# A transformer decoder on Trainium2: VectorE's and ScalarE's instruction orders fixed by hand in the attention stages, and side work placed anew

## The chip, the cores and the metric

The kernel runs on one core of one Trainium2 chip. The core has five engines that run their own instruction streams: TensorE (PE in the profile) multiplies matrices, VectorE (DVE) and ScalarE (ACT)[...], GpSimd (POOL) works on the large on-chip memory (SBUF), and SyncE (SP) issues transfers. TensorE's results land in PSUM[...]. The metric is the device time of one execution in microseconds (us); lower is better.

## The reference, cut to what matters

All numbers are fp32. The input `x` is 8 batches of 256 tokens of width 256. Six blocks are added to it, one after the other; the change touches the first four.

```python
x = x + self_attention_0(layernorm(x))        # 16 heads of 16, rotary q and k, biases
x = x + cross_attention_0(ctx, layernorm(x))  # queries are layernorm(x) itself, keys and values are
                                              # halves of ctx; keys beyond the batch's length masked
x = x + experts_0(layernorm(x))               # below
x = x + self_attention_1(layernorm(x))        # 16 heads of 16, rotary, causal
x = x + cross_attention_1(layernorm(x), ctx)  # 16 heads of 64, projections, a null key
x = x + experts_1(layernorm(x))               # top-1 gate of 8 experts of width 704, a shared one

def experts_0(x):                             # for each batch alone
    g = clip(x @ gate, 1e-6)                  # 256 tokens x 8 experts
    for _ in range(8):                        # sinkhorn, here without the logarithm
        g = g / g.sum(tokens); g = g / g.sum(experts)
    vals, idx = top_k(g.T, 32)                # each expert takes its 32 best tokens
    out[idx[e]] = (x[idx[e]] @ W[e]) * vals[e]   # scattered back; the last expert's entry stands
```

## The kernel before, in words

**Units and steps.** The stage that the change touches takes the first 548 us. It is cut into 24 units (L759 to L768). Units 0 to 15 go by pairs of batches: two `SelfAttention` of layer 0, then two `CrossAttention`. Units 16 to 23 are the causal `SelfAttention` of layer 1, one for each batch. Each unit has four steps: two halves `c` of the heads by two tiles `kt` of 128 keys. The main loop (L905 to L926) goes over units `n` and steps `k`. In each pass it calls `scores` of the next step, then `values` of this one, then the side work listed for `(n, k)`. TensorE runs the matmuls in just this order.

**A step.** `scores` makes four matmuls into `st`, whose PSUM pool `scp` has one buffer of four banks. Two exponentials on ScalarE then turn it into `pT` (L339); the next step's `st` can start only when both have read it. In the causal layer GpSimd sets half of each `pT` to zero behind the diagonal (`affine_select`, L344). `values` makes eight matmuls into `o` (L365). After an odd step `divided_T` (L385) runs on VectorE: a transpose to `by_q`, a reciprocal of the sums `dens`, a multiplication, a transpose into `attT`.

**What a self-attention unit needs around its steps.** `norm` takes statistics on VectorE, `rs` by a power on GpSimd (L258), and writes the two halves of `xn` on VectorE. `rows` transposes `xn` on TensorE (`tr`, L285), and ScalarE copies it to `xnT`. `heads(t)` projects half the tokens (`qk`) and turns q and k: VectorE multiplies by cosines (`qc`) and sines (`qs`, two instructions). In layer 0 GpSimd adds the turned bias to `qc`. The sum of `qc` and `qs` goes to `qkr`: for t=0 on GpSimd, for t=1 on VectorE (L460). `vals(t)` projects `v`, which ScalarE copies into `padv`. `begin` transposes `qkr`: keys (`tr`, copied by ScalarE to `kT`) and queries (`qps`, L472). `masked_queries` (L303) then writes `qps` twice with heads masked in turn: one half of `qm` on VectorE (L306), one on ScalarE (L307). `out(t)` projects `attT` (`ao`) and adds it to `x` on VectorE; in layer 0 GpSimd adds `offset` to `x` first. The side lists put all this one or two units ahead: for unit n, `norm` at (n-2, 2), `rows` at (n-2, 3), both `heads` at (n-1, 0), both `vals` at (n-1, 1), `begin` at (n-1, 2); `out` follows in unit n+1.

**What a cross-attention unit needs.** `norm` at (n-1, 0); GpSimd's copies of the values, `vals`, at (n-1, 1); `begin`, which transposes `xn` into `qps` and masks it, at (n-1, 2). `out` (`oR`) transposes `attT` back and adds it to `x`.

**The experts.** For each pair of batches the generator `chosen_experts` (L621) does the third block. It is advanced one piece at a time by `experts_at` (L846), whose numbers are pieces per step; the pair of units 4i to 4i+3 is treated in units 4i+5 to 4i+10, the last two pairs in fewer (13 to 17 and 16 to 20). Its pieces: rows normalised to `xnb` and transposed; logits `lg`; eight sinkhorn rounds (`cs` on TensorE, L649, then five small VectorE instructions that end at `g`, L659); the top 32 in four rounds of MAX8, FIND_INDEX8 and MATCH_REPLACE8 on VectorE (L670 to L674), written to DRAM and read back; `pick` on GpSimd (L699), `rps` on TensorE, a copy to `rT`; the expert matmuls `y`; `put` on GpSimd, `junk`, `weight` and `ys` on VectorE; `back` on TensorE, added to `x`.

**What sets the order.** [...] Only TensorE's order is the one written:

```python
order.enter_context(tc.manual_schedule(engines={mybir.EngineType.PE}))
```

For VectorE, ScalarE, GpSimd and SyncE a scheduler, when the program is built, picks the next instruction by its own estimate of what is ready and by priority. Five places raise the priority with `tc.high_priority(offset=SOON)`: the norms, `divided_T`, the experts' norms and the sinkhorn rounds. All small products share three PSUM buffers in the pool `mm` (L558).

**Start and end.** Before the loop come unit 0's `norm`, `turn` (the turned biases), `rows`, `heads` and `vals`, unit 1's `norm`, `load`, `key_tables`, `begin`, unit 1's `rows` and the first `scores`. At unit 1 `expert_tables` (L591) loads the experts and writes zeros to buffers in DRAM: `xs`, `ys`, `yo` and eight times a part of `packs`, all from GpSimd's queue. After (20, 3) `weights_x` (L772) loads 6 MB for the fifth block. After the loop `tables_x` (L797) makes small tables, among them `nvw`, and then comes the last unit's `out`.

Of the kernel before, what the change touches and what calls it, by code (L numbers as in the profile page):

```python
# [39 lines left out]
P = 128  # L40
# [17 lines left out]
SOON = 60  # L58
# [99 lines left out]
def plain(  # L158
# [144 lines left out]
    def masked_queries(work, ps, masks):  # L303

        qm = work.tile([P, 2, 2, S], F32, tag="qm", name="qm")
        nc.vector.tensor_scalar(qm[:, :, 0, :], ps, masks[:, 0:1], None, ALU.mult)  # L306
        nc.scalar.activation(qm[:, :, 1, :], ps, AF.Copy, scale=masks[:, 1:2])  # L307
        return qm

    class Core:  # L310
# [9 lines left out]
        def scores(self, step):  # L320


            c, kt, q0 = self.queries(step)
            n = S - q0
            st = scp.tile([P, 4, 2, S], F32, tag="sc", name="st")
            for r in range(4):
                rows = slice(HP * r, HP * r + HP)
                nc.tensor.matmul(  # L328
                    st[:, r, :, :n],
                    self.kT[rows, c, bass.ts(kt, P)],  # L330
                    self.qm[rows, c, :, q0:],
                    start=True,
                    stop=True,
                )
            pTs = []
            for k in range(2):
                pT = work.tile([P, 2, 2, S], F32, tag="pT", name="pT", bufs=4)
                kb = {} if self.bias is None else {"bias": self.bias[:, kt : kt + 1]}
                nc.scalar.activation(  # L339
                    pT[:, :, :, :n], st[:, 2 * k : 2 * k + 2, :, :n], AF.Exp, scale=self.scale, **kb  # L340
                )
                if self.causal:

                    nc.gpsimd.affine_select(  # L344
                        out=pT[:, :, :, :P],
                        in_=pT[:, :, :, :P],
                        compare_op=ALU.is_ge,
                        fill=0.0,
                        base=0,
                        pattern=[[0, 2], [0, 2], [1, P]],  # L350
                        channel_multiplier=-1,
                    )
                pTs.append(pT)
            self.exps[step] = pTs

        def values(self, step):
# [22 lines left out]
            if kt:  # L379
                with tc.high_priority(offset=SOON):  # L380
                    divided_T(self.attT[:, c, :], o, self.dens[:, c, :])
# [47 lines left out]
    class SelfAttention:  # L429
# [8 lines left out]

        def norm(self):
            with tc.high_priority(offset=SOON):  # L440
                self.xn = work.tile([P, 2, D], F32, tag="xn", name="xn")
                mv, rs = norm_stats([x[:, 2 * self.b + t, :] for t in range(2)], 1e-5, small, "ln")
                for t in range(2):
                    self.head = normed(self.xn[:, t, :], x[:, 2 * self.b + t, :], mv, rs, t)
# [9 lines left out]
        def heads(self, t):  # L454
            qk = mm.tile([P, 2 * D], F32, tag="mm", name="qk")
            self.projected(qk, t, 0, 2 * D)
            qc, qs = rotary(qk, t, self.layer, work)
            if self.bias is not None:
                nc.gpsimd.tensor_tensor(qc, qc, self.bias[0][:, t, :], ALU.add)
            (nc.vector if t else nc.gpsimd).tensor_tensor(self.qkr[:, t, :], qc, qs, ALU.add)  # L460
# [15 lines left out]

        def out(self, t):
            b, attT = self.b, self.core.attT
            xt = x[:, 2 * b + t, :]
            if self.bias is not None:  # L480
                nc.gpsimd.tensor_tensor(xt, xt, self.bias[1], ALU.add)
# [31 lines left out]
    class CrossAttention:  # L513
# [12 lines left out]

        def norm(self):
            with tc.high_priority(offset=SOON):
                self.xn = work.tile([P, 2, D], F32, tag="xn", name="xnx")
                mv, rs = norm_stats([x[:, 2 * self.b + t, :] for t in range(2)], 1e-5, small, "ln")  # L530
                for t in range(2):
                    normed(self.xn[:, t, :], x[:, 2 * self.b + t, :], mv, rs, t)
# [88 lines left out]
    def chosen_experts(b0, nb):  # L621
# [3 lines left out]
        def normed_rows(b):  # L625
            with tc.high_priority(offset=SOON):
                mv, rs = norm_stats([x[:, 2 * (b0 + b) + t, :] for t in range(2)], 1e-5, small, "ln")
                for t in range(2):
                    normed(xn[:, 2 * b + t, :], x[:, 2 * (b0 + b) + t, :], mv, rs, t)

        normed_rows(0)
        yield
        for b in range(nb):
            xnT = transposed(xn[:, 2 * b : 2 * b + 2, :], work, mm, "xnT")
# [6 lines left out]
            if b + 1 < nb:  # L641
                normed_rows(b + 1)
# [3 lines left out]
        for it in range(8):  # L646
# [3 lines left out]
            with tc.high_priority(offset=SOON):  # L650
                rc = bwork.tile([P, nb, E], F32, tag="rc", name="rc")
                nc.vector.reciprocal(rc, cs)
                nc.vector.tensor_tensor(g, g, rc.unsqueeze(2).to_broadcast([P, nb, 2, E]), ALU.mult)
                rsum = bwork.tile([P, nb, 2], F32, tag="rsum", name="rsum")
                nc.vector.tensor_reduce(rsum, g, AX.X, ALU.add)
                rr = bwork.tile([P, nb, 2], F32, tag="rr", name="rr")
                nc.vector.reciprocal(rr, rsum)
                dst = gt.rearrange("p t b e -> p b t e") if it == 7 else g
                nc.vector.tensor_tensor(dst, g, rr.unsqueeze(3).to_broadcast([P, nb, 2, E]), ALU.mult)  # L659
# [10 lines left out]
        for r in range(0, TOP, 8):  # L670
            nc.vector.max(top[:, 1, r : r + 8], v)
            nc.vector.max_index(place[:, r : r + 8], top[:, 1, r : r + 8], v)
            if r + 8 < TOP:
                nc.vector.match_replace(v, top[:, 1, r : r + 8], v, NEG)  # L674
        nc.vector.tensor_copy(top[:, 0, :], place)
# [162 lines left out]
    sides = {(n, k): [] for n in range(len(units)) for k in range(4)}  # L838

    def beside(n, k, *made):  # L840
        if n >= 0:
            sides[n, k] += made

    ex = [chosen_experts(2 * i, 2) for i in range(B // 2)]

    def experts_at(i, n, *counts):  # L846
        for k, m in enumerate(counts):
            beside(n, k, *[lambda: next(ex[i], None)] * m)

    for n, u in enumerate(units):  # L850
        if u.__class__ is SelfAttention:
            beside(n - 2, 2, u.norm)
            beside(n - 1, 0, partial(u.heads, 0), partial(u.heads, 1))
            beside(n - 1, 1, partial(u.vals, 0), partial(u.vals, 1))
            beside(n - 1, 2, u.begin)
            beside(n - 2, 3, u.rows)
            if u.layer:
                beside(n + 1, 2, partial(u.out, 0)) if n + 1 < len(units) else None
                beside(n + 1, 3, partial(u.out, 1)) if n + 1 < len(units) else None
            else:  # L860
                beside(n + 1, 0, partial(u.out, 0), partial(u.out, 1))
    for n, u in enumerate(units):
        if u.__class__ is CrossAttention:
            beside(n - 1, 0, u.norm)
            beside(n - 1, 1, u.vals)
            beside(n - 1, 2, u.begin)
            beside(n + 1, 0 if n == 15 else 2, u.out)
    beside(0, 1, add_up)
    beside(3, 3, slot_tables)
    for i in range(3):  # L870
        n = 4 * i + 5
        experts_at(i, n, 2, 2, 1, 1)
        experts_at(i, n + 1, *((1, 2, 2, 2) if i == 2 else (1, 1, 1, 1)))
        experts_at(i, n + 2, *((0, 1, 0, 0) if i == 2 else (0, 1, 1, 1)))
        if i < 2:
            experts_at(i, n + 3, 1, 0, 0, 1)
            experts_at(i, n + 4, 0, 1, 1, 1)
            experts_at(i, n + 5, 0, 1, 1, 1)
        else:
            experts_at(i, n + 3, 1, 1, 1, 1)  # L880
            experts_at(i, n + 4, 0, 1, 1, 1)
    experts_at(3, 16, 1, 1, 1, 1)
    experts_at(3, 17, 1, 2, 2, 2)
    experts_at(3, 18, 1, 1, 1, 0)
    experts_at(3, 19, 0, 1, 1, 2)
    experts_at(3, 20, 1, 2, 0, 0)

    units[0].norm()
    opening = ExitStack()
    opening.enter_context(tc.issue_after(units[0].head.ins))  # L890
    turn()
    order = ExitStack()
    order.enter_context(tc.manual_schedule(engines={mybir.EngineType.PE}))
    units[0].rows()
    for t in range(2):
        units[0].heads(t)
        units[0].vals(t)
    units[1].norm()
    for u in units[:2]:
        u.load()  # L900
    key_tables()
    units[0].begin()
    units[1].rows()
    units[0].core.scores(0)
    for n, u in enumerate(units):  # L905
# [8 lines left out]
        for k in range(4):  # L914
            if k < 3:
                u.core.scores(k + 1)
            elif n + 1 < len(units):
                units[n + 1].core.scores(0)
            u.core.values(k)
            for made in sides[n, k]:  # L920
                made()
            if (n, k) == (20, 3):
# [4 lines left out]
    wn, nvw, hot8 = tables_x(wd, wq_x, wout_x, nkrow, nvcol)  # L927
    order.close()
    for t in range(2):
        units[-1].out(t)  # L930
    first.close()
# [1881 lines left out]
```

## Time and profile before

| | |
|---|---|
| median of 3 runs | 1289.84 us (1289.42 to 1290.94) |
| profiled execution | 1294.03 us |
| its span, first to last instruction | 1292.3 us |
| mean TensorE clock granted | 0.971 of full |
| TensorE busy | 1171.2 us, 91% |
| VectorE, ScalarE, GpSimd busy | 582.7, 438.2, 374.4 us |
| first score matmul, last score matmul | 29.5 us, 529.4 us |
| first matmul of the next stage (`fm`) | 548.4 us |

The profile covers one execution. Busy time counts an engine's own work, not its waits; work of several engines overlaps, so the columns don't add to the span. In the table of stretches, each line begins with the window in us from the start and its length; then come the busy times of PE, PE's weight loads, DVE, ACT and POOL, each with a count of instructions, then the granted TensorE clock, the share of transfers, and GB/s. In the list of waits, a line names the instruction that waited, the one it waited for, and then the total in us, the count and the longest. In a timeline a line has the start and the duration in us, the engine, the source line, the operation, what it writes and reads (partitions by elements), how many instructions were put together, and in brackets the idle time before and what ended it.

### The profile page before, as it was taken

To read this page: it belongs to the slowest core of one execution; us is meant where nothing else is said; L and a number is where in the kernel's file an instruction comes from. 1 tells how busy PE (TensorE), PEld (TensorE's weight loads), DVE (VectorE), ACT (ScalarE), POOL (GpSimd) and SP (SyncE) were. 2 spreads that over 40 slices of the span, in tenths; PEclk is the share of its full clock that TensorE was granted. 3 is DMA by queue.
4 is the path that set the end of the run, shared out by engine and by line. 5 is a ranking of instruction groups with operands and counts; after the bars stand their busy time and mean duration, and the time that the engine had idled before them with its cause. 6 is when DMAs were issued, how large, how long until landed. Compare 5 with 4: busy or idle time off the path is not lost.

```text
span 1292.3 us, 28714 instructions
## 1 busy us (share of the span) xinstructions
PE 1171.2 (91%) x12188; PEld 721.7 (56%) x12188; DVE 582.7 (45%) x1632; ACT 438.2 (34%) x672; POOL 374.4 (29%) x450
## 2 busy tenths in 40 slices
PE   5877888978788879799999999999999999999996
PEld 2333344424344444356676666667676466888874
DVE  5455565765665765433343233324232657222213
ACT  2554554544432424213233232313142331122220
POOL 5322122332052434203242432414143504100014
PEclk8999998998998999899999999999999999999999
DMA  8990000000000032001110101020211205499934
GB/s 305 343 290 10 17 14 21 18 9 2 9 2 1 10 111 112 1 17 25 27 34 18 34 18 34 18 51 2 50 35 35 68 1 230 183 406 409 392 120 126
DMA packets 46923, 116.58 MB, mean 90 GB/s; under 512 B 8273, under 2 KB 30401, under 8 KB 42433
## 3 DMA queue, kind: packets, MB, share of 16 engines
q1 hardware_dynamic: 38912, 92.74, 21.1%
q0 software_dynamic: 5152, 18.89, 4.0%
q10 hardware_dynamic: 2720, 3.02, 0.7%
q8 instruction: 98, 1.61, 0.5%
q14 instruction: 41, 0.33, 0.1%
HBM read 104.00 MB, written 27.93 MB: 102 GB/s over the span
## 4 chain that ended last, share of the span: by engine, by line
PE 65%; DVE 5%; issue 3%; POOL 2%; ACT 2%; DMA 1%; SPq 0%; DVEq 0%; ACTq 0%; POOLq 0%
PE h L276 7%; PE v L276 6%; PE k L276 5%; PE ox L1423 4%; PE wo L276 4%; PE stx L1384 4%; PE out L1801 3%; PE h L1006 3%; PE out L1618 3%; PE st L328 3%; PE o L365 3%; PE q L276 2%; PE qk L276 2%; PE fm L276 2%; PE hx L1006 1%
## 5 line engine op out<-in xcount | busy, mean ns | idle before, releaser
L339 ACT ACTIVATE pT<-st 128x1024 f32<-128x1024 f32 (+1 forms) x128 | 110.4, 915 | 119.7 <-PE st L328 117.9
L365 PE MATMUL o<-pT,padv 128*32 128x256 f32 (+1 forms) x1536 | 104.9, 388 | 12.9 <-DVE by_q L390 7.3
L328 PE MATMUL st<-qm,kT 32*128 32x512 f32 (+1 forms) x512 | 73.8, 647 | 32.2 <-ACT qm L307 23.0
L365 PEld LDWEIGHTS o<-pT,padv 128*32 128x32 f32 x1536 | 42.1, 114 | 101.7 <-issue 48.9
L1390 POOL TENSOR_TENSOR both<-pTx 128x512 f32<-128x512 f32 x64 | 82.1, 1308 | 44.5 <-issue 38.9
L339 ACT ACTIVATE pT<-st,kbias 128x1024 f32<-128x1024 f32 x64 | 67.8, 1110 | 65.3 <-PE st L328 65.3
L276 PE MATMUL h<-xrT,w 128*64 128x128 f32 (+1 forms) x1936 | 87.3, 250 | 1.7 <-issue 1.7
L276 PEld LDWEIGHTS h<-xrT,w 128*64 128x64 f32 x1936 | 84.8, 137 | 4.4 <-issue 2.3
L1388 ACT ACTIVATE pTx<-stx 128x1024 f32<-128x1024 f32 x64 | 62.1, 1021 | 41.3 <-PE stx L1384 26.5
L999 DVE TENSOR_TENSOR midr<-sl,h 128x128 f32<-128x128 f32 x102 | 29.4, 288 | 101.8 <-PE h L276 67.6
L998 ACT ACTIVATE sl<-h 128x128 f32<-128x128 f32 (+1 forms) x114 | 35.3, 310 | 97.9 <-PE h L276 57.3
L1384 PE MATMUL stx<-qTx,kTx 64*128 64x256 f32 x512 | 64.3, 391 | 2.5 <-ACT pTx L1388 2.5
L276 PE MATMUL qk<-l_wqkv,xnT 128*64 128x512 f32 x256 | 62.1, 628 | 0.7 <-ACT xnT L288 0.7
L1423 PE MATMUL ox<-pTx,vx 128*64 128x256 f32 x512 | 62.3, 385 | 0.0
L258 POOL TENSOR_TENSOR lnrs<-lnve,mhalf 128x2 f32<-128x2 f32 x48 | 36.5, 772 | 88.4 <-DVE lnve L256 67.6
L344 POOL TENSOR_SCALAR_AFFINE_SELECT pT<-pT 128x512 f32<-128x512 f32 x64 | 42.4, 675 | 57.2 <-ACT pT L339 53.2
L390 DVE STREAM_TRANSPOSE by_q<-o 128x512 f32<-128x512 f32 x48 | 34.1, 711 | 54.6 <-PE o L365 54.6
L276 PE MATMUL wo<-wout_x,oT 128*64 128x256 f32 x512 | 58.0, 379 | 0.0
L1384 PEld LDWEIGHTS stx<-qTx,kTx 64*128 64x128 f32 x512 | 46.1, 186 | 20.3 <-ACT pTx L1388 7.2
L1478 POOL TENSOR_TENSOR oT<-oT,rs 128x512 f32<-128x512 f32 x30 | 37.3, 1274 | 66.1 <-DMA rs<-rd 66.1
L328 PEld LDWEIGHTS st<-qm,kT 32*128 32x128 f32 x512 | 21.9, 200 | 52.0 <-ACT qm L307 26.6
L258 POOL TENSOR_TENSOR lxrs<-lxve,mhalf 128x2 f32<-128x2 f32 x8 | 5.6, 702 | 154.9 <-DVE sc L1137 123.7
(366 smaller groups left out, 2179.0 us busy)
## 6 DMA issues: line engine op xcount, KB each, us to landing
w<-packs SPq DMA_DIRECT2D x22, 1408.0 KB
w<-packs SPq DMA_DIRECT2D x22, 768.0 KB
rs<-rd SPq DMA_DIRECT2D x16, 512.0 KB
packs<-L_ffn_w_eDF SPq DMA_DIRECT2D x8, 704.0 KB
packs<-L_ffn_w_eDF SPq DMA_DIRECT2D x8, 640.0 KB
packs<-L_ffn_w_eFD SPq DMA_DIRECT2D x8, 640.0 KB
ctxT<-ctx_T SPq DMA_DIRECT2D x8, 512.0 KB
wkv_x<-L_xattn_Wkv POOLq DMA_DIRECT2D x1, 4096.0 KB
```

Of the source, the lines that this page charges most:

```text
L258: nc.gpsimd.tensor_tensor(rs[:, :n], ve[:, :n], mhalf[:, :n], ALU.pow)
L276: nc.tensor.matmul(out[h], lhsT[:, h], rhs, start=start, stop=stop, skip_group_check=True)
L328: nc.tensor.matmul(st[:, r, :, :n], self.kT[rows, c, bass.ts(kt, P)], self.qm[rows, c, :, q0:], start=True, stop=True,)
L339: nc.scalar.activation(pT[:, :, :, :n], st[:, 2 * k : 2 * k + 2, :, :n], AF.Exp, scale=self.scale, **kb)
L344: nc.gpsimd.affine_select(out=pT[:, :, :, :P], in_=pT[:, :, :, :P], compare_op=ALU.is_ge, fill=0.0, base=0, pattern=[[0, 2], [0, 2], [1, P ...
L365: made = nc.tensor.matmul(o[HP * j : HP * j + HP, m, q0:], self.v_pad[:, kt, 8 * c + 2 * j + m, :], pTs[j // 2][:, j % 2, m, : S - q0], st ...
L1006: nc.tensor.matmul(h, shared["ws13"][:, c, lo : lo + P], shared["xnT"][:, c, bass.ts(q, 2 * S)], start=c == 0, stop=c == 1)
L1384: nc.tensor.matmul(st[:, g, kt, :], kT[rows, c, bass.ts(kt, P)], qT[rows, c, :], start=True, stop=True)
L1388: nc.scalar.activation(pT, st, AF.Exp, scale=scale)
L1390: nc.gpsimd.tensor_tensor(both, pT[:, :, 0, :], pT[:, :, 1, :], ALU.add)
L1423: nc.tensor.matmul(o[XD * g : XD * (g + 1), i, :], v[:, kt, 2 * (c2 + i) + g, :], pT[:, g, kt, :], start=kt == 0, stop=kt == 1, skip_group ...
L1618: nc.tensor.matmul(ps, mid[:, i, lo : lo + P], w2[:, i, :], start=i == 0, stop=i == NFC - 1)
```

## The change

The change alters no arithmetic. It does the following:

- VectorE's and ScalarE's orders are now the written ones too (`PINNED`); the five raised priorities go. GpSimd and SyncE stay with the scheduler.
- `qm` keeps its two masked halves apart: its layout is [mask, head half, tokens] where it was [head half, mask, tokens]; the score matmuls read it with a stride.
- Pieces of side work are split: `stats` from `norm`, `joined` (VectorE's addition for t=1) from `heads`, `biased` from `out`; the experts' generator yields after its statistics, after its norms and after each round of the top 32 but the last. Its transposed rows get a buffer of their own (`xnbT`).
- Side work has a position `at` within the step: `EARLY` runs before `values`, the rest after it, in order of `at`. For a self-attention unit `begin` moves from (n-1, 2) to (n-1, 1), `heads(0)` from (n-1, 0) to (n-2, 3), and one or both `vals` later; the experts' pieces get a written list of places.
- At the start unit 1's work moves behind the first `scores`; `weights_x` comes after (20, 1), and `tables_x` after the last `out`.

The diff, cut to its core:

```diff
-SOON = 60
+PINNED = {mybir.EngineType.PE, mybir.EngineType.DVE, mybir.EngineType.Activation}
...
         qm = work.tile([P, 2, 2, S], F32, tag="qm", name="qm")
-        nc.vector.tensor_scalar(qm[:, :, 0, :], ps, masks[:, 0:1], None, ALU.mult)
-        nc.scalar.activation(qm[:, :, 1, :], ps, AF.Copy, scale=masks[:, 1:2])
+        nc.vector.tensor_scalar(qm[:, 0], ps, masks[:, 0:1], None, ALU.mult)
+        nc.scalar.activation(qm[:, 1], ps, AF.Copy, scale=masks[:, 1:2])
...
-                    self.qm[rows, c, :, q0:],
+                    self.qm[rows, :, c, q0:],
...
-                with tc.high_priority(offset=SOON):
-                    divided_T(self.attT[:, c, :], o, self.dens[:, c, :])
+                divided_T(self.attT[:, c, :], o, self.dens[:, c, :])
...
-            (nc.vector if t else nc.gpsimd).tensor_tensor(self.qkr[:, t, :], qc, qs, ALU.add)
+            if not t:
+                nc.gpsimd.tensor_tensor(self.qkr[:, t, :], qc, qs, ALU.add)
+            self.parts = qc, qs
+
+        def joined(self):
+            nc.vector.tensor_tensor(self.qkr[:, 1, :], *self.parts, ALU.add)
...
-            xnT = transposed(xn[:, 2 * b : 2 * b + 2, :], work, mm, "xnT")
+            mv, rs = norm_stats([x[:, 2 * (b0 + b) + t, :] for t in range(2)], 1e-5, small, "ln")
+            yield
+            for t in range(2):
+                normed(xn[:, 2 * b + t, :], x[:, 2 * (b0 + b) + t, :], mv, rs, t)
+            yield
+        for b in range(nb):
+            xnT = transposed(xn[:, 2 * b : 2 * b + 2, :], bwork, mm, "xnbT")
...
                 nc.vector.match_replace(v, top[:, 1, r : r + 8], v, NEG)
+                yield
...
+    plan = {}
+
+    def beside(n, k, at, *made):
+        plan.setdefault((n, k), []).append((at, made))
+
+    def run(n, k, early):
+        for at, made in sorted(plan.get((n, k), ()), key=lambda p: p[0]):
+            if (at == EARLY) == early:
+                for one_made in made:
+                    one_made()
+
+    EARLY = 0
     for n, u in enumerate(units):
         if u.__class__ is SelfAttention:
-            beside(n - 2, 2, u.norm)
-            beside(n - 1, 0, partial(u.heads, 0), partial(u.heads, 1))
-            beside(n - 1, 1, partial(u.vals, 0), partial(u.vals, 1))
-            beside(n - 1, 2, u.begin)
-            beside(n - 2, 3, u.rows)
...
+            beside(n - 2, 1, 80, u.stats)
+            beside(n - 2, 2, EARLY, u.norm)
+            beside(n - 2, 2, 30, u.rows)
+            beside(n - 2, 3, 30, partial(u.heads, 0))
+            beside(n - 1, 0, 30, partial(u.heads, 1))
+            beside(n - 1, 1, 20, u.joined)
+            beside(n - 1, 1, 30, partial(u.vals, 0))
+            beside(n - 1, 1, 60, u.begin)
+            beside(*((n, 0, 40) if u.layer else (n - 1, 2, 30) if n % 4 else (n - 1, 3, 40)), partial(u.vals, 1))
+            beside(n, 3, 80, u.biased)
+            for t in range(2):
+                beside(n + 1, *((2 + t, 40) if u.layer else (0, 20 + t)), partial(u.out, t))
         else:
...
+            beside(n - 1, 0, 80, u.stats, u.vals)
+            beside(n - 1, 1, EARLY, u.norm)
+            beside(n - 1, 1, 60, u.begin)
+            beside(n + 1, *((2, 40) if n % 4 == 2 else (0, 20)), u.out)
...
+    begun = (-1, 3, 80), (0, 0, EARLY), (0, 0, 80), (0, 1, EARLY)
+    pieces = begun + (
+        (0, 3, 40), (1, 0, 70), (1, 2, 40), (1, 3, 40),
+        (2, 0, 70), (2, 1, 45), (2, 2, 10), (2, 2, 70), (2, 3, 70), (3, 0, 70), (3, 1, 45), (3, 2, 70),
+        (3, 3, 10), (4, 0, EARLY), (4, 0, 85), (4, 1, EARLY),
+        (4, 2, 70), (4, 3, 10), (5, 1, 10), (5, 2, 15), (5, 3, 10), (6, 1, 10), (6, 2, 15),
+    )
...
+        for n, k, at in (pieces, pieces, sooner, soonest)[i]:
+            beside(4 * i + 4 + n, k, at, partial(next, made, None))
...
+            order.enter_context(tc.manual_schedule(engines=PINNED))
+        u.rows()
+        u.heads(0)
+        if u is units[0]:
+            u.vals(0)
+            u.heads(1)
+            u.joined()
+            u.vals(1)
+            for v in units[:2]:
+                v.load()
+            u.begin()
+            u.core.scores(0)
+            key_tables()
...
+            run(n, k, True)
             u.core.values(k)
-            for made in sides[n, k]:
-                made()
-            if (n, k) == (20, 3):
+            run(n, k, False)
+            if (n, k) == (20, 1):
...
-    wn, nvw, hot8 = tables_x(wd, wq_x, wout_x, nkrow, nvcol)
     order.close()
     for t in range(2):
         units[-1].out(t)
+    wn, nvw, hot8 = tables_x(wd, wq_x, wout_x, nkrow, nvcol)
```

## The prediction

> **What bounds the kernel now.** I read the page's first part, then busy time by stretches, then TensorE's waits, then the timeline of single groups. Step (n,k) below is the loop's pass k in unit n, from one `st` on TensorE to the next.
>
> ```profile
> PE 1171.2 (91%) x12188; PEld 721.7 (56%) x12188; DVE 582.7 (45%) x1632; ACT 438.2 (34%) x672; POOL 374.4 (29%) x450
> ...
> 38.00:100.00 62.00, 49.05 (x484) 20.96 (x482) 32.67 (x81) 36.09 (x42) 16.89 (x22) 1.00 0.91 295
> ...
> 259.00:356.00 97.00, 76.21 (x762) 35.99 (x762) 62.39 (x215) 41.43 (x50) 20.92 (x26) 0.91 0.02 7
> ...
> 548.00:1292.00 744.00, 728.32 (x7894) 511.54 (x7894) 259.26 (x659) 203.47 (x370) 200.16 (x223) 1.00 0.29 101
> ```
>
> After 548 us TensorE hardly waits, and the change leaves that code alone. What can be won lies before: about 105 us of TensorE idle. Its waits from the first score matmul to the last:
>
> ```profile
> PE st L328 <- ACT qm L307: 29.1, 19, 5.3
> PE tr L285 <- DVE xnb L262: 14.6, 3, 4.9
> PE st L328 <- ACT pT L339: 14.3, 17, 2.1
> PE cs L276 <- DVE g L659: 11.6, 5, 4.5
> PE o L365 <- DVE by_q L390: 7.3, 5, 1.9
> ```
>
> Almost all are waits for the right order on VectorE (DVE) or ScalarE (ACT), whose busy shares are under half. A step without a stall:
>
> ```profile
> 100.04 1.14 PE L328 MATMUL st<-qm,kT 32*128 32x512 f32 x8 [0.31 <-ACT pT L339]
> 101.11 1.07 PE L365 MATMUL o<-pT,padv 128*32 128x256 f32 x16
> 102.11 3.65 PE L276 MATMUL qk<-l_wqkv,xnT 128*64 128x512 f32 x16
> 105.69 1.14 PE L328 MATMUL st<-qm,kT 32*128 32x512 f32 x8
> ```
>
> So starts lie 1.07 (`st`), 1.00 (`o`) and 3.58 us (`qk` for both t) apart. Likewise `v` or `ao` for one t is 0.94, `tr` 0.5 to 0.6, `qps` 0.44, `y` 1.9, `back` 1.78. A step also can't be shorter than `st`, a gap of 0.2 and two exponentials: 3.26 in self-attention (520.92 to 524.18), 3.44 in cross-attention. Adding each step's matmuls and taking the larger of sum and floor gives 405 us for the 94 steps from 29.5 to 529.4; they took 499.9. In most steps the sum is met within 0.02; the 95 us over it sit in some forty.
>
> [...] the sixth of the zeroing DMAs on GpSimd's queue waits below, and nothing passes it. [...] here ScalarE's `qm` waited 22 times for VectorE's, 24.0 us in all. [...] after the 4.78 us wait at 126.5, `st` took 2.09 instead of 1.14. [...] at 14.3, beside a GpSimd add, two `xn` took 1.91 instead of 0.73.
>
> **The change, part by part.** I take the changed order from the program as it is built; durations are from rows of before.
>
> *Masked halves apart*: nothing. In the changed program ScalarE's half still waits for VectorE's half[...]. Moving reads and writes keep their sizes. Zero from both sides.
>
> *k and q turned one group sooner* (`begin` from step 2 to step 1) and *levelled groups*: the sums of the 94 steps go from 386.8 to 383.9, with floors from 405 to 396: -9. The wait of `st` for `qm` (29.1) and most of that for `xnb` (14.6) go, as both are ready a step ahead. But `begin` now lies in an odd step, and the fixed order puts VectorE's part of that step as: four instructions of `divided_T` (1.95, from 219.85 to 221.80), `joined` (0.69), `qm`. The transposes need `joined`: it ends 2.8 after `o`, and TensorE has only one `v` (0.94) and two transposes (0.25). Wait 1.6, in ten of the fifteen self-attention steps; where `back` or `rps` lies between, none. Then statistics (1.3), GpSimd's power (0.85) and `xn` (0.8) follow `qm` in that queue, and the next step's `tr` comes 2.07 (1.64 in the causal layer) after `qps`, but `xn`'s first half only 3.4 after: a wait of 1.3 to 1.9 in some twelve steps. And `qm` stands before the next exponentials on ScalarE: those start up to 0.5 late, or 1.8 where VectorE does `divided_T` first (cross-attention).
>
> *Fixed order with the top-32 pieces.* One round of them, from the timeline:
>
> ```profile
> 185.47 0.42 DVE L671 MAX8 top<-v 16x8 f32<-16x256 f32 x1
> 185.92 0.08 DVE L672 MATCH_VALUE_LOAD place<-top,v 16x8 f32 x1
> 186.00 0.41 DVE L672 FIND_INDEX8 place<-top,v 16x8 uint32<-16x256 f32 x1
> 186.44 0.08 DVE L674 MATCH_VALUE_LOAD v<-top,v 16x8 f32 x1
> 186.52 0.40 DVE L674 MATCH_REPLACE8 v<-top,v 16x256 f32<-16x256 f32 x1
> 186.95 0.42 DVE L671 MAX8 top<-v 16x8 f32<-16x256 f32 x1
> ```
>
> A round is 1.48. In step (8,0) VectorE now gets two rounds, `xnb`, a residual, `qc`, `qs` and statistics, 7.3 us against 4.4 of TensorE, with about 3 left over from (7,3); in (8,1) 1.15 more, `xnb` and `divided_T` still stand before `joined`. Followed through, `joined` ends about 7 us after TensorE needs it. The same in (12,1) and (16,1), and 4.5 in (4,1). [...] about 2 us of the following matmuls are lost too. In (10,1) and (14,1) VectorE has 8.2 us for 4.85 of TensorE: the sinkhorn chain (1.14 from 222.31) ends behind `junk` and `ys`, and (10,2) waits 2.6, 1.2 and 0.9.
>
> *GpSimd's order* is left to the scheduler, and moved:
>
> ```profile
> 22.12 2.65 POOL L602 DMA_DIRECT2D packs<-zero  x5
> 31.36 0.52 POOL L602 DMA_DIRECT2D packs<-zero  x1 [6.59 <-DMA xs<-zero]
> 32.79 0.52 POOL L602 DMA_DIRECT2D packs<-zero  x1 [0.91 <-DMA ys<-zero]
> ```
>
> The power of unit 1's norm stood before these; now it stands behind the one that waits for `xs`. So `xn` of unit 1 comes at about 33.5 (before, it was ready at 16.2), and `tr` and `qk` stand ahead of the second `st` on TensorE. Step (0,0) ends at about 42.3 instead of 38.0: +4.3. Later four `pick` (3.65) that wait for their indices stand ahead of a power in (16,1) and of the masks in (19,0): 2.3 and 2.1. SP's queue keeps its order of loads; `weights_x` is two steps sooner, and its 6 MB still have some 69 us till their first use (74 before). The tail (`nvw` behind the last `ao`) has the same VectorE work before the next stage: zero, with 2 either way.
>
> The sum, stage by stage (before from the trace, after as walked):
> start to (0,0): 38.0, 42.3. To (3,3): 62.0, 64.4. Units 4 to 7: 75.0, 78.1. 8 to 11: 83.8, 88.8. 12 to (15,3): 97.1, 87.9, as that stage's waits for `g` (4.54, 1.60 and 1.74, and the clock behind them) go. To (20,3): 133.2, 128.7. Unit 21: 17.4, 19.0. 22: 17.6, 15.6. 23: 5.2, 5.8. Sum 529.3, 530.6: +1.3. I add 4, an estimate, for some twenty `xn` pairs on the path that meet GpSimd (row mean 500 ns against 370 used): +5. The profiled execution has a span of 1292.3 within 1294.03, and the median is 1289.84. The difference applied to the median: **1295 us**. The waits move rather than go.
>
> **Rivals.** *A, the queues keep up* (chance 0.33): VectorE is under 65% busy in every stretch, so its backlogs may be smaller than walked. The walked waits are 530.6 + 4 - 29.5 - 396 = 109; 4.3 of them are at the start and about 42 are the 1.6 and 1.3 to 1.9 ones with the late exponentials, so some 63 are backlogs. If all of these are absent: 1295 - 63 = 1232; if half: 1263. It decides once some 8 of the 63 are missing. Against it: each backlog is a sum of rows[...]. Its reach is 1225 to 1287.
> *B, GpSimd's queue holds more up* (0.19): masks, picks, puts and powers share it in units 16 to 20; it decides where one of the eight-per-unit masks comes more than 0.85 after its exponential, as `o` then waits (2.51 once before). At 0.5 us for each of 40 causal steps, +20: 1315; reach 1305 to 1325. This is slower too.
> *C, the fixed order does no more than the scheduler's* (within the forecast): if each move is hidden, nothing changes: 1290.
>
> **How the numbers follow.** The forecast, that the waits move, has 0.48 and reaches from 1287 to 1305. About 0.2% (2.6 us) is what a measurement can tell: 0.12 of it is within that of before and 0.36 above. With B slower is 0.55; A gives faster 0.33. The range leaves out the lower end of A (under 1250, 0.1) and B's upper end (over 1316, under 0.1).
>
> **What would show it.** TensorE's waits: `st` for `qm` under 8 us; `tr` for `qkr` by VectorE 30 to 50 us, with single waits over 5 at units 8, 12 and 16; `tr` for `xn` 15 to 25; (0,0) ending near 42. If `tr` for `qkr` is under 20 us, the VectorE walk is wrong and A holds. If `o` waits for GpSimd over 15 us, B holds. ScalarE's `qm` should still wait for VectorE's. The stretch after the last `ao` should be 744 us as before; if it isn't, something unseen moved.

## The result, and the profile after

The changed kernel takes 1319.51 us (1318.59 to 1321.26, 4 runs) against 1289.86 (1289.42 to 1290.94): a ratio of 1.023, with a 95% interval of 1.0213 to 1.0248. It is 29.7 us slower. The forecast was 1295 and its range ended at 1316, so the sign was right and the size was not. The profiled execution took 1318.59, with a span of 1316.9; before, 1294.03 with 1292.3. The spans differ by 24.6. The other 5 us lie in the base: the profiled execution of before was 4.2 above its median, that of after 0.9 below.

The page's first part for the changed kernel:

```profile
PE 1179.2 (90%) x12188; PEld 720.5 (55%) x12188; DVE 593.6 (45%) x1632; ACT 437.4 (33%) x672; POOL 370.4 (28%) x450
```

Everything up to the next stage's first matmul, `fm`, in the kernel before:

```profile
0.00:548.40 548.40, 443.25 (x4297) 210.34 (x4297) 323.81 (x975) 234.70 (x302) 174.42 (x228) 0.93 0.23 75
```

The same in the changed kernel, and its units 16 to 20 alone:

```profile
0.00:575.40 575.40, 451.88 (x4296) 210.84 (x4296) 334.89 (x975) 233.65 (x302) 170.36 (x228) 0.91 0.22 72
...
369.47:514.37 144.90, 115.88 (x1137) 58.30 (x1135) 88.14 (x259) 46.14 (x72) 54.18 (x75) 0.91 0.15 53
```

TensorE ran the same 12188 matmuls. From `fm` to its last matmul it took 734.3 us, against 734.6 before; what follows the last matmul is 2.2 shorter (7.1 against 9.3), which was not looked into. So the loss is all in the first stage: `fm` starts at 575.4 where it started at 548.4, +27.0. Up to there TensorE was busy 451.9 us (443.3 before) and idle 123.5 (105.1). So 18.4 us are more waiting, and 8.6 are the same matmuls run slower, at a lower mean granted clock (0.91 against 0.93). TensorE's waits from the first score matmul on, as the list of waits has them (total, times, longest):

```profile
PE tr L285 <- DVE qkr L465: 40.6, 14, 6.5
PE tr L285 <- DVE xn L262: 35.0, 16, 8.5
PE st L328 <- ACT pT L339: 12.2, 10, 2.5
PE cs L276 <- DVE g L664: 7.7, 6, 2.5
...
PE o L365 <- POOL pT L344: 2.4, 3, 1.6
```

The waits of `st` for `qm` (29.1) are gone but for 1.6 at the start, those of `tr` for `xnb` (14.6) are gone, and `o` no longer waits for `by_q` (7.3). In their place stand 75.6 us of `tr` waiting for two VectorE products. The times from step to step on TensorE, summed by stage, show where the forecast and the trace part:

| stage | before | forecast | measured |
|---|---|---|---|
| start to the end of (0,0) | 38.0 | 42.3 | 43.25 |
| to (3,3) | 62.0 | 64.4 | 69.71 |
| units 4 to 7 | 75.0 | 78.1 | 78.89 |
| units 8 to 11 | 83.9 | 88.8 | 88.73 |
| units 12 to 15 | 97.0 | 87.9 | 88.89 |
| units 16 to 20 | 133.2 | 128.7 | 144.90 |
| unit 21 | 17.4 | 19.0 | 22.92 |
| unit 22 | 17.6 | 15.6 | 15.63 |
| unit 23, to the last `st` | 5.2 | 5.8 | 5.96 |
| last `st` to `fm` | 19.0 | 19.0 | 16.5 |

### The profile page after: what moved, and what is told of

The parts are those of the page before. It is cut to its first block, busy times and chain, and to the rows that moved or that the text cites. A ratio compares the mean times of both kernels' runs of the same rounds, so it can differ in the third digit from the quotient of the medians.

```text
span 1316.9 us, 28731 instructions
## 1 busy us (share of the span) xinstructions
PE 1179.2 (90%) x12188; PEld 720.5 (55%) x12188; DVE 593.6 (45%) x1632; ACT 437.4 (33%) x672; POOL 370.4 (28%) x450
## 4 chain that ended last, share of the span: by engine, by line
PE 65%; DVE 12%; issue 5%; POOL 3%; ACT 2%; DMA 1%; SPq 0%; POOLq 0%; ACTq 0%; DVEq 0%
PE h L276 6%; PE v L276 5%; PE k L276 5%; PE ox L1436 4%; PE wo L276 4%; PE stx L1397 4%; PE st L328 3%; PE out L1814 3%; PE out L1631 3%; PE h L1019 3%; PE o L365 3%; PE q L276 2%; PE qk L276 2%; PE fm L276 2%; PE tr L285 2%
## 5 line engine op out<-in xcount | busy, mean ns | idle before, releaser
L1401 ACT ACTIVATE pTx<-stx 128x1024 f32<-128x1024 f32 x64 | 62.2, 1022 | 41.6 <-PE stx L1397 26.5
L276 PE MATMUL qk<-l_wqkv,xnT 128*64 128x512 f32 x256 | 66.0, 638 | 1.4 <-ACT xnT L288 1.4
L285 PE MATMUL tr<-ident,xn 128*128 128x128 f32 x96 | 19.5, 325 | 44.0 <-DVE xn L262 42.9
L285 PE MATMUL tr<-ident,qkr 128*128 128x128 f32 x64 | 15.0, 322 | 43.7 <-DVE qkr L465 43.5
```

The source lines that it names most:

```text
L276: nc.tensor.matmul(out[h], lhsT[:, h], rhs, start=start, stop=stop, skip_group_check=True)
L285: nc.tensor.transpose(ps[:, c, t * P : (t + 1) * P], rows[:, t, c * P : (c + 1) * P], ident)
L1401: nc.scalar.activation(pT, st, AF.Exp, scale=scale)
```

## The experiments

The theory, V: VectorE is not short of time; its fixed queue puts work ahead of what TensorE needs. Its main rival, P: the new places themselves are at fault, since k, q and `xn` fall due sooner whatever order VectorE has. The kernel before took 1288.27 to 1293.39 us in the medians of four chips, so ratios to that kernel on the same chip are compared; the changed kernel's is 1.023, and 0.001 of ratio is 1.3 us.

### VectorE's order given back to the scheduler

```diff
-PINNED = {mybir.EngineType.PE, mybir.EngineType.DVE, mybir.EngineType.Activation}
+PINNED = {mybir.EngineType.PE}
```

> The changed kernel with only TensorE's order fixed; VectorE's and ScalarE's are the scheduler's again, the raised priorities stay out. Theory V (TensorE's waits come from what stands ahead in VectorE's fixed queue): the waits of tr for qkr and xn fall from 40.6 + 35.0 us to under 30, and the time to 1275-1295. Rival P (the new places of the side work are at fault, since k, q and xn fall due sooner whatever the order on VectorE): the waits stay above 60 us and the time above 1310.

Measured: 1262.24 us, ratio 0.9743 (0.9691 to 0.9795). The time is below the range expected. The new places with VectorE and ScalarE free are faster than the kernel before by 2.6%; the fixed orders take that and 2.3% more. The waits for `qkr` fall from 40.6 to 8.0, and those for `xn` leave the list's upper part. TensorE's idle time up to `fm` is 75.5 us. P falls: the places gain.

How one step differs shows it best. First the changed kernel's TensorE in (8,1), then its VectorE ahead of the wait's end:

```profile
199.46 0.44 PE L285 MATMUL tr<-ident,qkr 128*128 128x128 f32 x2
206.37 0.69 PE L285 MATMUL tr<-ident,qkr 128*128 128x128 f32 x2 [6.47 <-DVE qkr L465]
206.86 1.06 PE L477 MATMUL qps<-ident,qkr 128*128 128x128 f32 x4
207.84 2.09 PE L328 MATMUL st<-qm,kT 32*128 32x512 f32 x8
```

```profile
198.72 0.73 DVE L420 TENSOR_TENSOR qs<-qk,sin_pairs 128x256 f32<-128x256 f32 x2
199.39 0.40 DVE L253 BATCH_NORM_STATS2 lnst<-x 128x6 f32<-128x256 f32 x1
...
200.65 0.41 DVE L676 MAX8 top<-v 16x8 f32<-16x256 f32 x1
...
203.18 0.72 DVE L262 TENSOR_SCALAR xnb<-x,lnmv,lnrs 128x256 f32<-128x256 f32 x2
203.83 0.70 DVE L389 STREAM_TRANSPOSE by_q<-o 128x512 f32<-128x512 f32 x1
...
205.67 0.65 DVE L465 TENSOR_TENSOR qkr<-qc,qs 128x512 f32<-128x512 f32 x1
```

Of the two operands of `qkr`, `qs` is there at 199.45, and GpSimd's addition to `qc` runs from 198.88 for 1.28. The sum could be made at 200.2; it is made at 205.67, because the end of the statistics, two rounds of the top 32, `xnb` and `divided_T` stand ahead of it, all of them less urgent. In the run with VectorE free, the same unit's step:

```profile
180.98 0.74 DVE L420 TENSOR_TENSOR qs<-qk,sin_pairs 128x256 f32<-128x256 f32 x2
181.64 1.31 DVE L262 TENSOR_SCALAR xnb<-x,lnmv,lnrs 128x256 f32<-128x256 f32 x2
182.87 0.68 DVE L465 TENSOR_TENSOR qkr<-qc,qs 128x512 f32<-128x512 f32 x1
183.47 0.70 DVE L389 STREAM_TRANSPOSE by_q<-o 128x512 f32<-128x512 f32 x1
```

GpSimd's addition ends at 182.5 here, and `qkr` follows at 182.87, ahead of `by_q`; the rounds were done at 178.6.

### ScalarE's order kept fixed, VectorE's free

```diff
+PINNED = {mybir.EngineType.PE, mybir.EngineType.Activation}
```

> The changed kernel with TensorE's and ScalarE's orders fixed and VectorE's left to the scheduler. V: as with TensorE alone, within 5 us of it, as ScalarE's order costs nothing. If ScalarE's fixed order costs by itself (qm ahead of the exponentials), it is 5 to 15 us slower than that, with st waiting for pT more than 12 us. P: above 1310.

Measured: 1261.20 us, ratio 0.9743 (0.9689 to 0.9796), the same as with TensorE alone; `st` waits for `pT` 13.4 us in both. ScalarE's order, with `qm` ahead of the exponentials, costs nothing that shows. What parts this run from the changed kernel is VectorE's order alone.

### The written order on VectorE, in the places of before

```diff
-    order.enter_context(tc.manual_schedule(engines={mybir.EngineType.PE}))
+    order.enter_context(tc.manual_schedule(engines={mybir.EngineType.PE, mybir.EngineType.DVE}))
```

> The kernel before, with VectorE's order fixed as written as well as TensorE's; places as before. V in its wide form (the written order on VectorE costs in either set of places, since what is written later but ready sooner can't pass): slower than before by 30 us or more, 1320 to 1370, with waits for qkr, xn or by_q over 50. V in its narrow form (it costs only where begin stands in the step of divided_T and joined, as in the change): within 15 of before, under 1305.

Measured: 1343.29 us, ratio 1.0415 (1.0379 to 1.0451). The wide form holds: 4.2% of the time of before is lost in the old places, 4.9% in the new ones (0.9743 to 1.023). The waits are others, though: `xnb` 29.3, `cs` for `g` 21.0, `o` for `by_q` 13.5, `qm` 29.6. So the loss doesn't hang on where `begin` stands. Not all of it is made in VectorE's own queue: GpSimd's order, still the scheduler's, moves with it. With VectorE free, GpSimd makes unit 1's power at 19.50, ahead of the zeroing transfers that wait, and not at 32.31 behind them (there its operand is ready at 24.72, but GpSimd first stands idle 8.56 for the transfer ahead of it); (0,0) ends at 35.13 instead of 43.25.

### The raised priorities left out, nothing else

```diff
-                with tc.high_priority(offset=SOON):
+                if True:
```

(at all five places)

> The kernel before with the five raised priorities left out and nothing else; TensorE's order fixed, places as before. If the new places make the 28 us that the changed kernel gains with VectorE's order free: no faster than before, 1288 to 1310. If leaving out the priorities makes them: 1255 to 1275.

Measured: 1298.00 us, ratio 1.0036 (1.0016 to 1.0056): a little slower. In the old places leaving them out gains nothing. The gain with VectorE free therefore comes with the rest of the change, the new places above all; the split pieces and the buffer `xnbT`, which come with them, were not tried apart.

### The layout of qm alone

```diff
-        nc.vector.tensor_scalar(qm[:, :, 0, :], ps, masks[:, 0:1], None, ALU.mult)
+        nc.vector.tensor_scalar(qm[:, 0], ps, masks[:, 0:1], None, ALU.mult)
```

(with ScalarE's half and the score matmuls to match, in the kernel before)

> The kernel before with only the new layout of qm. As predicted: no difference, 1290 within 2.6 us, ScalarE's qm still waiting for VectorE's about 24 us in all. If the layout frees ScalarE's half from VectorE's, those waits fall under 5 us, st waits less for qm, and the time falls to 1280-1286; if the strided read is slow, st takes over 1.14 us for its eight matmuls and the time rises by 64 times that.

Measured: 1293.76 us, ratio 1.0005 (0.9982 to 1.0028). ScalarE's `qm` still waits for VectorE's 25.0 us in all (24.0 before), and `st` has its median of 587 ns in both. No difference.

### joined ahead of divided_T

```diff
-            beside(n - 1, 1, 20, u.joined)
+            beside(n - 1, 1, EARLY, u.joined)
```

> The changed kernel with the addition for t=1 (joined) put ahead of values in its step, so ahead of divided_T on VectorE. V: the ten waits of 1.1 to 1.5 us of tr for qkr go and those at (8,1), (12,1), (16,1), (20,1) fall by 1.95 to about 4.5; the sum falls from 40.6 to about 20, and the time by 15 to 22, to about 1300. P, or if xn takes over the waits: less than 5 us off, 1315 or more.

Measured: 1307.86 us, ratio 1.0088 (1.0052 to 1.0124), some 18 us of the 29.7 back. The waits for `qkr` fall from 40.6 to 8.7, in (8,1) to 2.86, further than expected. Those for `xn` stay (35.1), and in (20,1) a wait of 6.4 for the addition of `back` takes the place of the 5.9 for `qkr`. Of the single mends tried, this line gives back the most.

### k and q turned no sooner than before

```diff
-            beside(n - 1, 1, 60, u.begin)
+            beside(n - 1, 2, 60, u.begin)
```

(self-attention only)

> The changed kernel with begin back at step 2 of the unit ahead, so k and q are turned no sooner than before; all orders stay fixed. V: the addition for t=1 has a step more, the waits of tr for qkr fall from 40.6 to under 12, those for xn from 35.0 to about 20, as qm no longer stands ahead of the statistics; st waits for qm 8 to 20 instead of 0; 1285 to 1300. If the sooner turning is worth more than it costs (the waits for qm come back in full, 29), the time stays at 1310 or more.

Measured: 1324.13 us, ratio 1.028 (1.0255 to 1.0305), slower still. Of V's expectation only the waits for `qkr` came true. The time lies where the other reading put it, with the waits for `qm` at 23.2 of the 29 that it named. The first waits of this run:

```profile
PE tr L285 <- DVE xn L262: 42.1, 16, 8.7
PE st L328 <- ACT qm L307: 23.2, 16, 1.6
PE o L365 <- DVE by_q L389: 16.1, 5, 4.6
```

None for `qkr` is left, as expected. But VectorE's backlog in (8,0) and (8,1) is still there, and now `o` waits 3.80 for `by_q` in (8,2). The sooner turning isn't the cause; the backlog meets whatever TensorE asks for next.

### The transposes of xn one step later

```diff
-            beside(n - 2, 2, 30, u.rows)
+            beside(n - 2, 3, EARLY, u.rows)
```

> The changed kernel with rows (the transposes of xn) one step later on TensorE, ahead of values of step 3, with VectorE's order unchanged. V with the clock: the 26 us of waits for xn after the start fall under 8 and what the halved clock costs after them goes too: 1285 to 1297. V without the clock (a wait costs only its own length): 1300 to 1304. If qk then waits for the copy to xnT or the waits go elsewhere: 1310 or more.

Measured: 1312.96 us, ratio 1.0184 (1.0153 to 1.0216), some 6 us back where V had expected 16 at the least. The waits for `xn` fell from 35.0 to 9.8, of which 8.9 are at the start. But:

```profile
PE cs L276 <- DVE g L664: 13.2, 5, 3.8
PE qk L276 <- ACT xnT L288: 12.3, 13, 1.4
```

`qk` now follows so closely that it waits for the copy, thirteen times, and `cs` waits 5.5 more. Most of these waits moved.

### Three rounds of the top 32 behind joined

```diff
-        (3, 3, 10), (4, 0, EARLY), (4, 0, 85), (4, 1, EARLY),
+        (3, 3, 10), (4, 1, 70), (4, 1, 72), (4, 1, 74),
```

> The changed kernel with three of the four rounds of the top 32 (for the first three pairs) put behind joined, qm and the statistics in VectorE's queue, at the end of steps (8,1), (12,1), (16,1). V: 4.45 us of work leaves the queue ahead of joined, so those three waits fall from 6.5 to about 2.0 and the sum for qkr from 40.6 to 27; 1300 to 1308 with the clock. If the read back of the indices then comes late, cps waits up to 4 us each time and the time stays above 1312.

Measured: 1331.27 us, ratio 1.0324 (1.0295 to 1.0353), 12 us worse. In (8,1) the wait fell only from 6.47 to 4.43: with the rounds gone, VectorE stood idle 0.81 twice, each time with `xnb` at the head of its queue waiting for GpSimd's power. Then the indices came back late, and `cps`, which takes them up on TensorE, waited 5.06 in (8,2). Less work in the queue is not the same as the needed piece sooner.

### Unit 1's statistics ahead of the zeroing transfers

```diff
     for u in units[:2]:
-        u.stats()
+        if u is units[0]:
+            u.stats()
...
             u.heads(1)
+            units[1].stats()
             u.joined()
```

> The changed kernel with unit 1's statistics ahead of unit 0's joined on VectorE, so that GpSimd's power for them comes ahead of the zeroing transfers in its queue. V: the wait of tr for xn at 33.57 (8.5) goes, step (0,0) ends at 36 to 39 instead of 43.25, and the time falls by 4 to 7, to 1313-1316. If the wait goes to another engine (qk for t=0 of unit 1 behind the same transfers): less than 2.

Measured: 1314.06 us, ratio 1.0189 (1.0172 to 1.0206), 5 us back. The wait of 8.5 for `xn` is gone and (0,0) ends at 33.87, 9.4 sooner; the next stretch, to (4,0), is 4.5 longer, as in (0,1) `tr` now waits 1.79 for GpSimd's `qkr` and 1.51 for VectorE's, and (2,0) is 2.2 longer.

### nvcol loaded at unit 2

```diff
             nc.sync.dma_start(wo1, a["l1_wo"].rearrange("(c p) f -> p c f", p=P))
+            for g in range(2):
+                nc.sync.dma_start(nvcol[XD * g : XD * (g + 1), :], a["L1_xattn_null_kv"][1:2, :].rearrange("o d -> d o"))
```

(and the same load taken out of `weights_x`). The reason is VectorE's queue of the changed kernel in (20,1):

```profile
492.83 0.27 DVE L825 TENSOR_REDUCE own<-ident 128x2 f32<-128x128 f32 x1
499.36 0.16 DVE L826 TENSOR_TENSOR own<-own,nvcol 128x2 f32<-128x2 f32 x1 [6.26 <-DMA nvcol<-L_xattn_null_kv]
499.44 0.71 DVE L389 STREAM_TRANSPOSE by_q<-o 128x512 f32<-128x512 f32 x1
...
501.87 0.67 DVE L465 TENSOR_TENSOR qkr<-qc,qs 128x512 f32<-128x512 f32 x1
```

`own` belongs to `tables_x`, which is written after the loop and outside the fixed order. The scheduler slots such work between the fixed instructions where it holds it to be ready; `weights_x`, now two steps sooner, had just issued the load.

> The changed kernel with the small vector nvcol loaded at unit 2 instead of in weights_x at (20,1), so that VectorE's own has it; all orders fixed as in the change. V: own waited 6.3 us for this transfer in VectorE's queue ahead of divided_T and joined; the wait of tr for qkr in (20,1) falls from 5.9 to under 1.5 and the time by 5 to 8 with the clock, to 1311-1315. If joined were late there for another reason (back's addition to x ahead of it): less than 2 off.

Measured: 1312.42 us, ratio 1.017 (1.0134 to 1.0206), some 8 us back; (20,1) takes 5.89 instead of 12.19. (The profiled execution, 1316.90, was the slowest of its four, so its trace shows less of the gain.)

> Both: only TensorE's order fixed, and nvcol loaded at unit 2. The same wait stood there in the run with TensorE's order alone (qps waited 5.4 for back's addition to x). V: 1254 to 1258, 4 to 8 below that run. If the scheduler's order changes elsewhere with it: 1262 or more.

With VectorE free as well: 1248.55 us (1247.00 to 1249.37), ratio 0.9675 (0.9641 to 0.9710). It beats both kernels: 3.2% under the kernel before, and by ratio some 9 us under the run with TensorE's order alone, more than expected (the ends of the two intervals overlap). (20,1) takes 5.41 where it took 11.53. In the run with TensorE's order alone `own` had waited 6.62 for the same transfer, ahead of `by_q`: this wait is not a cost of the fixed order, as the scheduler set it too.

### TensorE kept busy through the long waits

```diff
     def begin(self):
+            qps = mm.tile([P, 2, S], F32, tag="mm", name="qps")
+            if self in [units[n] for n in (9, 13, 17, 21)]:
+                for _ in range(22):
+                    for c in range(2):
+                        nc.tensor.matmul(qps[:, 0, bass.ts(c, P)], ident, ones, start=True, stop=True)
```

> The changed kernel with 44 matmuls of 128x128 that nobody reads put on TensorE ahead of the waits for qkr in (8,1), (12,1), (16,1) and (20,1), about 4.9 us each, so that TensorE isn't idle there. Clock as a cost of its own[...]: the waits fall from 6.5 to about 1.6, the st after them take 1.14 instead of 2.09, and the time falls by 4 to 9, to 1311-1315. If the wait costs its own length alone: no change, 1319 within 2.

Measured: 1329.48 us, ratio 1.0298 (1.0231 to 1.0364). The fill was mis-sized: the 44 matmuls show as 88 records and took 10.1 us, longer than the waits, so the time doesn't tell the two readings apart. Hence half as many, `range(11)`:

> The changed kernel with 22 matmuls of 128x128 that nobody reads, 5.0 us by the run with 44, ahead of the waits for qkr in (8,1), (12,1), (16,1) and (20,1); shorter than the waits, so only TensorE's idleness changes. Clock as a cost of its own: qps after them takes 0.60 instead of 1.06, the steps (8,1) with (8,2) take 13.9 instead of 15.75, the time falls by 4 to 8, to 1311-1315. If a wait costs its own length alone: no change, within 2 of the changed kernel's 1319.5.

Measured: 1318.09 us, ratio 1.0194 (1.0164 to 1.0225). By ratio that is 4.6 us below the changed kernel, but the two intervals overlap, and 1318.09 also lies within 2 of 1319.5, as the other reading had it: the time doesn't decide. The trace is plainer. TensorE in (8,1):

```profile
199.04 5.18 PE L477 MATMUL qps<-ones,ident 128*128 128x128 f32 x44
...
206.24 0.60 PE L481 MATMUL qps<-ident,qkr 128*128 128x128 f32 x4
206.77 1.14 PE L328 MATMUL st<-qm,kT 32*128 32x512 f32 x8
```

Without the fill, `qps` took 1.06 and `st` 2.09 (above). (8,1) and (8,2) together take 14.28 us instead of 15.75, though `qkr` is no sooner, and (12,1) with (12,2) do the same. But (16,1) with (16,2) take 20.10, as without the fill (20.06), since there the next wait, for `xn`, grows from 2.56 to 4.41; and (20,1) with (20,2) take 17.86 for 18.11. So a wait of 6.5 us cost about 1.5 more in slow matmuls at two of the four places; at the other two little or nothing was won.

### GpSimd's order fixed as well

```diff
+PINNED = {mybir.EngineType.PE, mybir.EngineType.Pool}
```

(VectorE and ScalarE free, `nvcol` early)

> The run with TensorE's order alone and nvcol early (1248.6), with GpSimd's order fixed as written as well. Rival B in the small (GpSimd's free order holds masks back): the wait of o for pT of 4.5 in (19,1) goes, 1238 to 1245. If the written order costs on GpSimd as it does on VectorE (picks and copies of values that wait ahead of masks and powers): 1255 or more, with waits of o for pT or tr for xn over 20.

Measured: 1279.43 us, ratio 0.9899 (0.9861 to 0.9936), 29 us worse than without. Both expectations hold in part. The wait of `o` for the mask in (19,1) is gone, and units 16 to 20 take 115.67 instead of 121.82. But in (1,1) `qpsx`, the cross-attention's `qps`, waits 22.98 at one stroke: GpSimd's power for it now stands behind the zeroing transfers, of which one waited 7.36 and the next 8.31 for transfers issued before them. A kernel with those transfers elsewhere wasn't tried.

## Why the prediction was wrong, point by point

**Right, by its own signs.** `tr` for `qkr` was to be 30 to 50 us with single waits over 5 at units 8, 12 and 16: it is 40.6, with 6.47, 6.49 and 6.52 (at (4,1) it is 3.27 where 4.5 was walked). `st` for `qm` under 8: 1.6. (0,0) near 42: 43.25, with `xn` of unit 1 at 33.57 as walked. ScalarE's `qm` still waits for VectorE's, 47.2 us in 24 times. The masked halves are worth nothing, shown alone. The walk of VectorE's queue gave units 8 to 15 within 1.1 us. Rival A (the queues keep up) fell, since `qkr` is over 20. Rival B (GpSimd holds up the masks) fell, since `o` waits 2.4 where over 15 was its mark.

**Wrong: "To (20,3): 133.2, 128.7".** It is 144.90. Up to the last `st` the forecast's lines sum to +1.3, and the trace shows +29.5. Of these 28.2 us this line holds 16.2, "To (3,3)" 5.3 and unit 21 3.9. (The whole span misses by less, 24.6 for 5: 4 had been added to the sum for GpSimd, and some 5 came off behind the last `st`.) In this line three things were left out or sized too small.

- *"`weights_x` is two steps sooner, and its 6 MB still have some 69 us till their first use."* The first use was `own`, which the walk didn't look for inside the loop because it is written after it. It held VectorE 6.3 us in (20,1); loading `nvcol` early took 4.5 us off this stage in the trace, and some 8 off the time. The profile of before had shown it, with a wait of 2.78 where the prediction counted 74 us of room:

```profile
477.70 0.16 DVE L820 TENSOR_TENSOR own<-own,nvcol 128x2 f32<-128x2 f32 x1 [2.78 <-DMA nvcol<-L_xattn_null_kv]
```

- *"The next step's `tr` comes 2.07 (1.64 in the causal layer) after `qps`, but `xn`'s first half only 3.4 after: a wait of 1.3 to 1.9 in some twelve steps."* In the causal layer it is 2.74, 2.12 and 2.12 at (17,2), (18,2) and (19,2). (The 2.56 in (16,2) is the wait behind four `pick` on GpSimd, walked as 2.3.) The forecast of 15 to 25 us for `xn` became 35.0; 8.5 of that is the start, which the walk had but the sign left out, so the rest, 26.5, is just over it.
- *"about 2 us of the following matmuls are lost too."* The prediction took this only after the waits that it walked as long (7 and 4.5 us). In the profile of before, `tr`, `st` and `o` behind the wait of 4.78 us took 4.78 more from start to start, and 2.65 in the next step, so 2.1 were lost there. That shorter waits cost no clock was an assumption of the author's, and no trace showed it. In the changed kernel's trace a wait of 2.47 was enough; from 84.08 to 90.91 us the granted clock was 0.50:

```profile
84.53 1.11 PE L285 MATMUL tr<-ident,xn 128*128 128x128 f32 x4 [2.47 <-DVE xn L262]
85.57 2.09 PE L328 MATMUL st<-qm,memk 32*128 32x512 f32 x8
87.59 1.94 PE L365 MATMUL o<-pT,padv 128*32 128x256 f32 x16
```

`st` takes 1.14 and `o` 1.07 in an undisturbed step. In the run with half the fill the same wait, in the same step, cost no clock at all:

```profile
85.11 0.76 PE L285 MATMUL tr<-ident,xn 128*128 128x128 f32 x4 [2.48 <-DVE xn L262]
85.81 1.14 PE L328 MATMUL st<-qm,memk 32*128 32x512 f32 x8
```

Nor does a shorter one decide it: in the changed kernel a wait of 1.44 in (3,2) was followed by full speed (`st` 1.14), and one of 1.44 in (15,2) by half (`st` 1.80, `o` 1.94). The profile of before had such a case too, after a wait of 2.05:

```profile
396.76 0.41 PE L276 MATMUL cs<-g,ones 128*64 128x16 f32 x8 [2.05 <-DVE weight L742]
397.10 1.10 PE L328 MATMUL st<-qm,kT 32*128 32x256 f32 x8
398.14 1.94 PE L365 MATMUL o<-pT,padv 128*32 128x256 f32 x16
```

The same fault is about half of "To (3,3)" (69.71 for 64.4): (2,2) waits 2.47, and (2,3) then runs 2.6 over its sum. In the run with half the fill, whose fill comes only later, this stage took 67.39. How much of the 16.2 belongs to each of the three was not settled: the run without `own`'s wait gave 4.5 back in this stage, and the run with the transposes of `xn` a step later 4.7; for the clock alone this stage gives no clean figure (with half the fill it took 148.97, as other waits grew).

**Unit 21, 19.0 for 22.92.** Between `qm` and the end of the statistics that unit 23 needs, VectorE did statistics for the next stage, written outside the fixed order. `tr` waited 2.79 for `xn`. This is read from the queue's order, and wasn't tried apart.

**The base.** The difference of spans was put on the median as it was; the profiled execution of before stood 4.2 above its median, as the table of times showed. A +5 that was right would still have measured about +10.

**What the forecast didn't ask.** It weighed the change as a whole, and came to "the waits move". In fact two large effects of opposite sign met: the new places gain 2.6%, the fixed order on VectorE loses 4.9%. The walk had both within it, but its sum was a small difference of large terms. A sum of +1.3 can't carry a sign when single lines miss by up to 16: that the time rose, as forecast, is in part luck, as most of the terms missed happened to be losses.

## What to carry to other kernels

Before an engine's order is fixed by hand, split the change: the same places with that engine free, and the same order in the old places. Here one engine's order turned a gain of 2.6% into a loss of 2.3%. In a fixed queue, ask of each piece that another engine waits for what stands between its operands and it; and look for work from outside the fixed part, which the scheduler slots in where it sees room. Moving one piece in such a queue often moves the wait: of the single mends, four gave back 5 to 18 us and two lost. Whether the four add up, and so whether a fixed order can match the scheduler's here, was not tried.

## What the runs showed of the hardware that was not expected

- The length of a wait alone didn't decide whether TensorE ran at half speed after it: in one step, (2,2), a wait of 2.47 us was followed by half speed in the changed kernel (`st` 2.09) and one of 2.48 by full speed in the run with half the fill (`st` 1.14). What decided it was not shown. In the changed kernel's trace the granted clock was 0.50 in 17 stretches, and all of their starts lie a whole number of 3.413 us apart: 125.04, 203.55 and 363.97, for example, lie 12, 35 and 82 times that behind 84.08.
- A wait of 6.5 us cost about 1.5 us beyond its length at two places, (8,1) and (12,1): in the run with half the fill (8,1) and (8,2) took 14.28 instead of 15.75. At (16,1) filling it won nothing (20.10 for 20.06), as the next wait grew from 2.56 to 4.41.
- In the fill, matmuls in fp32 of 128x128 by 128 columns show as two records each, 88 for 44, one every 115 ns (118 in the fill half as long).
- The engines' orders differed in weight: ScalarE's, fixed or free, made no difference (0.9743 both), VectorE's 4.9% (0.9743 to 1.023), GpSimd's 2.2% (0.9675 to 0.9899), most of that in one wait (22.98 of 29 us).
